# Attention's output: a first sum and difference in halves at four places, and one rotation of queries moved

## Chip, cores, metric

One core of one Trainium2 chip. The time is device microseconds of one execution of the whole program, a single launch; the kernel before has three runs. The five engines are PE (TensorE matmul; PEld are its weight loads), DVE (VectorE), ACT (ScalarE), POOL (GpSimd) and SP (SyncE, which issues most transfers).

## The reference, cut to what matters

The program is four layers over x of 64 sequences of 32 tokens of 512. The change lies in the third layer's attention; the others are untouched.

```python
q = jnp.einsum('bsd,ed->bse', x, Wq).reshape(bsz, seqlen, HQ, D)   # 32 query heads of 128
k = ...                                                            # 8 key heads
v = ...
q = _rope(_rmsnorm(q, q_norm_w), pos)
k = _rope(_rmsnorm(k, k_norm_w), pos)
kc = k_cache[block_table].reshape(bsz, L, HK, D)                   # 512 cached keys per sequence
...
scores = jnp.where(valid[:, None, None, :], jnp.einsum('bqhd,bkhd->bhqk', q, k_all) * SCALE, -1e+30)
probs = jax.nn.softmax(scores, axis=-1)
o = jnp.einsum('bhqk,bkhd->bqhd', probs, v_all).reshape(bsz, seqlen, HQ * D)
return jnp.einsum('bse,de->bsd', o, Wo)
```

## The kernel before, in words

All arithmetic is in fp32. The 2048 tokens are 16 tiles of 128 rows (four sequences each). Attention runs over two halves of the heads, and in each half over the 16 tiles: 32 steps. Two steps make a pair, 16 pairs in all (0 to 15). A step has 16 turns (four sequences times four key heads), a pair 32 turns, and a turn two half steps, so that a pair has half steps 0 to 63.

A turn i does this: PE transposes the probabilities of turn i (`prT_ps`, four matmuls, L1094), and ACT copies them (`prT`, L1423). PE forms the scores of turn i+2 (L1401). DVE adds the mask and takes the minimum (L1406), ACT takes the exponent (L1410), DVE the reciprocal of the sum (L1412), and DVE scales the probabilities (`pr`, L1415). PE multiplies the values with the transposed probabilities (`po`, L1099). Once per sequence DVE forms a mask (L1393) and copies the sequence's own keys (`kt`, L1119), and POOL issues four indirect gathers of values (`vt`, L1125). After two sequences `own_part` adds the tokens' own values and writes the output of four heads' groups into `oT`, a tile of 128 x 16 x 128 per step (L1462 to L1465, on ACT and DVE).

Between these steps two other products are spread over a pair's half steps, by lists of places in the code. `at(i, f)` puts a function at half step i.

- The projections of the next pair (`Projections`): three groups g (keys and values, then two of queries) of seven products m each, in the order 1, 2, 5, 6, 3, 7, 4. Two tiles are taken together as two-by-two blocks with seven products instead of eight. Where a product completes 512 columns of queries or keys, they are normed and rotated (`rotated`): a square on ACT (L1158), on DVE a reduction (L1161), a scaling (L1162) and three multiplications (L1176 twice, L1179), on POOL an addition (L1180), a power (L130) and a multiplication (L1181). For queries the rotation is put off by `WAIT[m]` half steps (`put_off`). Later PE transposes the result (`turned`, L1094, `qkT_ps`), at half steps 37, 43, 51, 53 and so on.
- The output projection of the pair before (`Outputs`), again with seven products over two tiles. With o11, o12 the two halves of the first tile's heads, and o21, o22 those of the second, the products need o21 + o22 (`o_sum`, first read by m = 5 at half steps 16 and 17), later o_sum - o11 and o12 - that (`next_sum`, on DVE, at 17 and 26), and o11 - o21, which is written over o21 (read by m = 7 at half steps 32 and 33). Each operand has 128 x 8 x 128 numbers, and each product runs as two halves u of four of the eight. The first sum and difference are `first_sums` (L1331 and L1332), on POOL, at half step 0 of the next pair. After the last pair they are on DVE.

```python
WAIT = {2: 2, 3: 0, 7: 2, 4: 4}
...
ats = ((2, 4, 10, 12, 14, 18, 20), (22, 28, 30, 34, 36, 38, 40), (42, 44, 46, 50, 52, 54, 58))
...
at(i, partial(p.product, g, m), partial(later.append, next_wp))
```

These lists give the order in which the code issues its instructions. PE's order is tied to it (`on_pe`). On the other engines the framework that the kernel is written in plans the order itself, from the dependencies and buffers and with the code's order as priority, except where `issue_after` ties an instruction behind another: the square of a rotation is tied behind the last prT copy issued before it. Tiles come from pools with a number of buffers (`oT` three, `o_sum` one, masks two, tables of cosines and sines two of each name).

Of the kernel before, what the change touches and what calls it, by code (L numbers as in the profile page):

```python
# [28 lines left out]
ALU = mybir.AluOpType  # L29
# [1024 lines left out]
def attention(c, known, x_in, y_part, y_out, sums, tail):  # L1054
# [15 lines left out]
    tc, nc, a = c.tc, c.nc, c.a  # L1070
    half = HD // 2
    n_c = L // P
    with ExitStack() as outer:
# [64 lines left out]
        WAIT = {2: 2, 3: 0, 7: 2, 4: 4}  # L1138
# [62 lines left out]
        class Projections:  # L1201
# [76 lines left out]
            def turned(self, g, i, n):  # L1278
                r = self.c.pop((g, i, n)).rearrange("p (h d) -> p h d", d=HD)
                pt = transposes("tq", "qkT_ps", [r[:, m, :] for m in range(REP)])  # L1280
                if g == 0:
                    self.kT[i] = qp.tile([P, HKP, P], F32, name="kT_own", bufs=3)
                    nc.scalar.copy(self.kT[i], pt)
                    return
                if i not in self.qT:
                    self.qT[i] = qp.tile([P, HKP, SEQ, REP, S], F32, name="qT", bufs=3)
                nc.scalar.copy(self.qT[i][:, 2 * (g - 1) + n].rearrange("p j h s -> p h j s"),
                               pt.rearrange("p h (j s) -> p h j s", j=SEQ))
# [3 lines left out]
        KH = HQP // 2  # L1292
        QH = KH // 2
# [21 lines left out]
        class Outputs:  # L1315
# [7 lines left out]
            def first_blocks(self):  # L1323
                self.blocks = [(o[:, :KH, :], o[:, KH:, :]) for o in (oTs[2 * self.n],)]

            def first_sums(self, engine):
                self.o = [oTs.pop(2 * self.n + i) for i in range(2)]
                (_, _), (o21, o22) = self.blocks = [(o[:, :KH, :], o[:, KH:, :]) for o in self.o]
                self.s = qp.tile([P, KH, P], F32, name="o_sum", bufs=1)
                for q in (slice(0, KH),) if engine is nc.gpsimd else (slice(0, QH), slice(QH, KH)):  # L1330
                    engine.tensor_tensor(self.s[:, q], o21[:, q], o22[:, q], ALU.add)  # L1331
                engine.tensor_tensor(o21, self.blocks[0][0], o21, ALU.subtract)  # L1332

            def next_sum(self, m, u):
                (o11, o12), _ = self.blocks
# [148 lines left out]
        per = SEQ * HKP  # L1484
        GROUPS = tuple(range(HKP))

        def of(i):
            s, j, g = turns[i]
            h, T = steps[s]
            return s, h, SEQ * T + j, g  # L1490
# [31 lines left out]
        later, to_come, waiting = [], {}, {}  # L1522
# [91 lines left out]
        for s, (h, T) in enumerate(steps):  # L1614
            if s:
                oTs[s] = qp.tile([P, HQP, P], F32, name="oT", bufs=3)
            slots = [[] for _ in range(2 * per)]
            n = s // 2
            last_pair = n == len(outputs) - 1

            def at(i, *fs):
                to_come.setdefault(s * 2 * per + i, []).extend(fs)

            if s % 2 == 0:
                if s == 0:
                    p = projections[0]
                    at(1, partial(p.turned, 2, 0, 1), partial(own_keys, 0, 1, p.kT[0]))
                    for i, f in zip((3, 7, 11, 15), held):  # L1630
                        at(i, f)
                    for i, what in ((13, (1, 1, 1)), (15, (1, 1, 0)), (19, (2, 1, 1)), (25, (2, 1, 0))):
                        at(i, partial(p.turned, *what))
                if not last_pair:
                    p = projections[n + 1]
                    if n == 0:
                        ats = ((12, 14, 16, 17, 18, 20, 22), (24, 26, 28, 32, 33, 34, 38),
                               (40, 42, 44, 48, 49, 52, 56))
                        then = ((0, 0, 0, 21), (0, 1, 0, 29))
                        for i, f in zip((3, 5, 6, 7, 10), (partial(p.x, 0), partial(p.x, 1), p.x_sums,  # L1640
                                                           partial(p.tables, "k"), partial(p.tables, "q"))):
                            at(i, f)
                    else:
                        ats = ((2, 4, 10, 12, 14, 18, 20), (22, 28, 30, 34, 36, 38, 40),
                               (42, 44, 46, 50, 52, 54, 58))
                        then = ((0, 0, 0, 13), (0, 1, 0, 27))
                        at(3, partial(p.tables, "q"))
                    for *what, i in (*then, (1, 0, 0, 37), (1, 0, 1, 43), (1, 1, 1, 51), (1, 1, 0, 53),
                                     (2, 0, 0, 57), (2, 0, 1, 65), (2, 1, 1, 67), (2, 1, 0, 73)):
                        at(i, partial(p.turned, *what))  # L1650
                    for g in range(GB):
                        for m, i in zip(p.ORDER, ats[g]):
                            at(i, partial(p.product, g, m), partial(later.append, next_wp))
                            if g and m != 1 and m != 5 and m != 6:
                                at(i, partial(put_off, s * 2 * per + i + 1 + WAIT[m], waiting))
                    if n + 2 < len(projections):
                        then = projections[n + 2]
                        for i, f in zip((30, 40, 59, 61, 62), (then.load, partial(then.tables, "k"),
                                                               partial(then.x, 0), partial(then.x, 1),
                                                               then.x_sums)):  # L1660
                            at(i, f)
                else:
                    for i, f in zip((6, 14, 38, 46, 54), tail.weights(xp, wk, op, wp_tile)):
                        at(i, f)
                    at(43, tail.scaled)
                    for m, i in enumerate((45, 48, 49, 61)):
                        at(i, partial(tail.fold, ps, m))
                    at(44, begin_tail)
                    at(58, partial(load_tail, "y", 2, 4))
                    for i, tag in enumerate(("sc", "pt")):  # L1670
                        at(62, partial(turn_tail, i, tag))
                    at(52, outputs[n].first_blocks)
                    for i, where in enumerate((52, 54, 57, 59)):
                        at(where, partial(outputs[n].product, i), partial(later.append, next_wo))
                if n:
                    out = outputs[n - 1]
                    at(0, partial(out.first_sums, nc.gpsimd))
                    if out.h:
                        at(14, out.befores)
                    ats = (0, 1, 5, 9, 13, 16, 17, 21, 25, 29, 32, 33, 37, 41) if last_pair else \  # L1680
                        (0, 1, 6, 8, 16, 17, 24, 26, 32, 33, 48, 49, 56, 60)
                    for i, where in enumerate(ats):
                        at(where, partial(out.product, i), partial(later.append, next_wo))
                        if i in (5, 7):
                            for u in range(2):
                                at(where, partial(out.next_sum, 6 if i == 5 else 3, u))
                    at(47 if last_pair else 63, out.store)
                else:
                    for i in (40, 46, 52, 58):
                        at(i, next_wo)  # L1690
            for at in range(2 * per):
                slots[at].extend(to_come.pop(s * 2 * per + at, []))
            for t in range(per):
                i = s * per + t
                _, _, b, g = of(i)
                if last_pair and not prTs:
                    prTs[:] = [qp.tile([P, D], F32, name="projected", bufs=6).rearrange("p (n k) -> p n k", k=P)
                               for _ in range(2)]
                prT = turned(i)
                if g == HKP - 1:  # L1700
                    own_prTs = ([] if b % 2 == 0 else own_prTs) + [own_turned(b)]
                slot(waiting.pop(2 * i, []) + slots[2 * t])
                start(i + 2)
                if g == 1:

                    keys_of(i - 1 + 2 * HKP)
                slot(waiting.pop(2 * i + 1, []) + slots[2 * t + 1])
                to_finish.append(partial(finish, s, i, b, g, prT, own_prTs))
                while len(to_finish) > int(last_pair and i + 1 < len(turns)):
                    to_finish.pop(0)()  # L1710
        out = outputs[-1]
        out.befores()
        out.first_sums(nc.vector)
        load_tail("x", 0, 1)
        for i, tag in enumerate(("sc", "pt")):
            tail.choose(i, tag)
# [540 lines left out]
```

## Time and profile before

| | us |
|---|---|
| median of 3 runs | 3447.67 |
| lowest, highest | 3445.36, 3448.77 |
| the profiled execution | 3450.86 |
| its span, first to last instruction | 3449.1 |
| PE busy | 3402.2 (99%) |
| DVE, ACT, POOL busy | 2184.1, 1626.7, 1650.1 |
| POOL: the first sum, 15 times | 2.36 each (median) |
| POOL: the first difference, 15 times | 2.34 each (median) |
| DVE: mask, 128 times | 0.50 median, 3.01 longest |

The granted TensorE clock was 1.0. Attention's turns begin at 1033 us and end at about 3277 us. Busy times are of one execution; matmuls overlap one another, so that PE's share says that it hardly ever stands still, not that it could do no more. In the lists of groups a line of `at(...)` never shows: the line given is that of the helper which issues the instruction (L1094 for transposes, L1099 for products, L130 for the power).

### The profile page before, as it was taken

Reading aid. Unit: us, or ns where it says so; the run is one execution under the profiler, and the core shown is the slowest. Engines: PE = TensorE matmul, PEld = TensorE weight load, DVE = VectorE, ACT = ScalarE, POOL = GpSimd, SP = SyncE. Lnnn points to the kernel's source line nnn. Section 1 sums busy time; section 2 is a strip of 40 time slices with the busy share of each in tenths; the row PEclk is TensorE's granted clock in tenths of the full one; section 3 lists DMA queues with packets and bytes.
Section 4 is the critical chain, followed back from the end, with each engine's and each line's share of the span. In section 5 each row is a group of like instructions: output and inputs, shape, how many; then the busy total and the mean of one; then the engine's idle time right before and its main releaser. Section 6 shows DMA issues by size and latency. Waiting matters only on the chain.

```text
span 3449.1 us, 66979 instructions
## 1 busy us (share of the span) xinstructions
PE 3402.2 (99%) x21124; PEld 2673.1 (78%) x21124; DVE 2184.1 (63%) x5432; ACT 1626.7 (47%) x4260; POOL 1650.1 (48%) x1647
## 2 busy tenths in 40 slices
PE   8999999999999999999999999999999999999999
PEld 6556888888857777778787777777877778777788
DVE  5454534334457676766767767677676777767477
ACT  6332222222226655555555555555555555555522
POOL 0112433333337655655556455565564655645233
PEclk9999999999999999999999999999999999999999
DMA  5013555545467888888887888878788888887731
GB/s 211 25 52 122 191 160 169 167 156 163 149 224 227 251 255 247 260 262 252 259 256 255 256 252 260 260 252 270 247 256 269 256 265 259 254 255 241 253 104 63
DMA packets 631937, 740.28 MB, mean 215 GB/s; under 512 B 64546, under 2 KB 480290, under 8 KB 631586
## 3 DMA queue, kind: packets, MB, share of 16 engines
q1 hardware_dynamic: 580130, 562.94, 52.4%
q0 software_dynamic: 51456, 173.05, 14.3%
q8 instruction: 172, 2.82, 0.3%
q14 instruction: 179, 1.47, 0.1%
HBM read 689.61 MB, written 46.14 MB: 213 GB/s over the span
## 4 chain that ended last, share of the span: by engine, by line
PE 84%; DVE 6%; DMA 4%; issue 3%; ACT 1%; SPq 1%; POOL 1%; DVEq 0%; POOLq 0%; ACTq 0%
PE po L1099 12%; PE sc L1401 11%; PE py L1099 10%; PE pq L1099 9%; PE prT_ps L1094 6%; PE pkv L1099 5%; PE pz L615 4%; PE pd L276 4%; PE acc_a L615 4%; PE acc L1839 3%; PE acc_c L615 2%; PE qkT_ps L1094 2%; PE po L615 1%; PE acc_b L615 1%; PE acc_a L281 1%
## 5 line engine op out<-in xcount | busy, mean ns | idle before, releaser
L1125 POOL DMA_INDIRECT vt<-in_v_rows,v_rows x512 | 516.5, 1009 | 312.2 <-PE po L1099 187.4
L1410 ACT ACTIVATE pr<-pr,low 128x544 f32<-128x544 f32 x512 | 383.3, 749 | 543.8 <-DVE low L1406 541.9
L1401 PE MATMUL sc<-kt,qT 128*128 128x288 f32 (+1 forms) x2048 | 554.2, 393 | 8.1 <-DMA kt<-in_kT 4.9
L1401 PEld LDWEIGHTS sc<-kt,qT 128*128 128x128 f32 x2048 | 384.4, 190 | 222.5 <-issue 127.5
L1099 PE MATMUL po<-prT,vt 128*128 128x128 f32 x3840 | 508.6, 275 | 2.2 <-ACT prT L1423 0.6
L1099 PEld LDWEIGHTS po<-prT,vt 128*128 128x128 f32 x3840 | 488.4, 192 | 27.6 <-ACT prT L1423 10.6
L1406 DVE CUSTOM_DVE_ANT_0 pr<-sc,mask 128x544 f32<-128x544 f32 x512 | 368.4, 720 | 143.7 <-PE sc L1401 143.5
L1180 POOL TENSOR_TENSOR projected<-projected,swapped 128x512 f32<-128x512 f32 x160 | 208.5, 1303 | 297.4 <-DVE projected L1179 274.9
L1415 DVE TENSOR_SCALAR pr<-pr,low 128x512 f32<-128x512 f32 x512 | 319.5, 624 | 12.6
L1094 PE MATMUL prT_ps<-ident,pr 128*128 128x128 f32 x2048 | 311.4, 275 | 4.9 <-DVE pr L1415 4.8
L1423 ACT COPY prT<-prT_ps 128x512 f32<-128x512 f32 x480 | 275.6, 574 | 18.7 <-PE prT_ps L1094 11.3
L1412 DVE RECIPROCAL low<-low 128x1 f32<-128x1 f32 x512 | 82.2, 160 | 319.2 <-ACT pr L1410 318.6
L1094 PEld LDWEIGHTS prT_ps<-ident,pr 128*128 128x128 f32 x2048 | 236.7, 141 | 15.4 <-issue 7.2
L1099 PE MATMUL py<-wo,oT 128*128 128x256 f32 x1024 | 241.8, 379 | 0.0
L1099 PE MATMUL pq<-wp,x_sums 128*128 128x512 f32 x512 | 240.2, 593 | 0.0
L1099 PEld LDWEIGHTS py<-wo,oT 128*128 128x128 f32 x1024 | 186.4, 190 | 21.1
L130 POOL TENSOR_TENSOR rs<-rs,minus_half 128x4 f32<-128x4 f32 x160 | 179.9, 1125 | 30.3 <-DVE low L1412 18.8
L1413 ACT ACTIVATE own_pr<-pr,low 128x32 f32<-128x32 f32 x512 | 164.9, 322 | 43.8 <-DVE low L1412 40.9
L1099 PE MATMUL pq<-wp,xT 128*128 128x512 f32 x384 | 180.6, 593 | 1.1 <-DVE projected L1269 1.1
L1099 PE MATMUL py<-wo,o_sum 128*128 128x256 f32 x768 | 181.2, 379 | 0.2 <-issue 0.2
L1132 ACT COPY own_vt<-v 32x128 f32<-32x128 f32 x512 | 150.8, 295 | 58.0 <-PE po L1099 42.4
L1181 POOL TENSOR_TENSOR projected<-projected,rs 128x512 f32<-128x512 f32 x160 | 172.0, 1075 | 8.1
(378 smaller groups left out, 6529.9 us busy)
## 6 DMA issues: line engine op xcount, KB each, us to landing
kt<-in_kT SPq DMA_DIRECT2D x2048, 64.0 KB
wp<-in_sums SPq DMA_DIRECT2D x192, 512.0 KB
wo<-out_sums SPq DMA_DIRECT2D x128, 512.0 KB
wp<-in_WqT SPq DMA_DIRECT2D x96, 512.0 KB
wo<-in_WoT SPq DMA_DIRECT2D x96, 512.0 KB
down1T<-in_down1T SPq DMA_DIRECT2D x80, 256.0 KB
wp<-in_WkT SPq DMA_DIRECT2D x32, 512.0 KB
xt<-x SPq DMA_DIRECT2D x48, 256.0 KB
```

The lines of the kernel that those rows point to most:

```text
L130: self.nc.gpsimd.tensor_tensor(t, t, self.minus_half[:, :n], ALU.pow)
L615: c.on_pe(nc.tensor.matmul(out, lhsT, rhs, start=start, stop=stop, skip_group_check=more))
L1094: c.on_pe(nc.tensor.transpose(pt[:, m, :], piece, c.ident))
L1099: c.on_pe(nc.tensor.matmul(out, lhsT, rhs, start=first and i == 0, stop=last and i == len(pairs) - 1))
L1125: nc.gpsimd.indirect_dma_start(out=vts[b % 2][:, n, :], out_offset=None, in_=a["v_rows"], in_offset=bass.IndirectOffsetOnAxis(ap=rows[h][: ...
L1180: last_turn.append(nc.gpsimd.tensor_tensor(src, src, tmp, ALU.add).ins)
L1181: last_scaled.append(nc.gpsimd.tensor_tensor(src, src, rs.unsqueeze(2).to_broadcast([P, REP, HD]), ALU.mult).ins)
L1401: c.on_pe(nc.tensor.matmul(sc[:, lo + n * PSIZE:lo + m * PSIZE].rearrange("p (n k) -> p n k", k=PSIZE), q, kt[:, n:m, g, :], start=True, s ...
L1406: ins = nc.vector.tensor_tensor_reduce(pr[:, :NK], sc[:, lo:lo + NK], masks[h, b], -SCALE, 3.0e38, ALU.add, ALU.min, low[:, 0:1]).ins
L1410: nc.scalar.activation(pr[:, :NK], pr[:, :NK], AF.Exp, bias=low[:, 0:1], scale=-1.0, accum_out=low[:, 1:2])
L1415: nc.vector.tensor_scalar(pr[:, :L], pr[:, :L], low[:, 2:3], None, ALU.mult)
L1423: last_prT.append(nc.scalar.copy(prT, pt).ins)
```

## The change

The first sum and the first difference are each formed in two halves of four of the eight blocks, as separate functions, and put at half steps 2 and 5 (sums) and 19 and 22 (differences) instead of both whole at half step 0. After the last pair, on DVE, the difference is formed in halves too. Beside it, the rotation of the queries that product (g, m) = (1, 3) completes is put off by two half steps instead of none (to half step 39 instead of 37), in all pairs but the first (and the last, which has no projections).

```diff
-            def first_sums(self, engine):
+            def all_blocks(self):
                 self.o = [oTs.pop(2 * self.n + i) for i in range(2)]
-                (_, _), (o21, o22) = self.blocks = [(o[:, :KH, :], o[:, KH:, :]) for o in self.o]
+                self.blocks = [(o[:, :KH, :], o[:, KH:, :]) for o in self.o]
                 self.s = qp.tile([P, KH, P], F32, name="o_sum", bufs=1)
-                for q in (slice(0, KH),) if engine is nc.gpsimd else (slice(0, QH), slice(QH, KH)):
-                    engine.tensor_tensor(self.s[:, q], o21[:, q], o22[:, q], ALU.add)
-                engine.tensor_tensor(o21, self.blocks[0][0], o21, ALU.subtract)
+
+            def first_sum(self, u, engine):
+                o21, o22 = self.blocks[1]
+                q = slice(u * QH, (u + 1) * QH)
+                engine.tensor_tensor(self.s[:, q], o21[:, q], o22[:, q], ALU.add)
+
+            def first_difference(self, u, engine):
+                q = slice(u * QH, (u + 1) * QH)
+                engine.tensor_tensor(self.blocks[1][0][:, q], self.blocks[0][0][:, q], self.blocks[1][0][:, q],
+                                     ALU.subtract)
...
-                                at(i, partial(put_off, s * 2 * per + i + 1 + WAIT[m], waiting))
+                                wait = 2 if n and (g, m) == (1, 3) else WAIT[m]
+                                at(i, partial(put_off, s * 2 * per + i + 1 + wait, waiting))
...
-                    at(0, partial(out.first_sums, nc.gpsimd))
+                    at(0, out.all_blocks)
+                    for u in range(2):
+                        at(2 + 3 * u, partial(out.first_sum, u, nc.gpsimd))
+                        at(19 + 3 * u, partial(out.first_difference, u, nc.gpsimd))
...
         out.befores()
-        out.first_sums(nc.vector)
+        out.all_blocks()
+        for u in range(2):
+            out.first_sum(u, nc.vector)
+        for u in range(2):
+            out.first_difference(u, nc.vector)
```

## Prediction, made before the changed kernel ran

> **What bounds the kernel now.** I read the page first: the busy times, then the chain that ended last.
>
> ```profile
> span 3449.1 us, 66979 instructions
> PE 3402.2 (99%) x21124; PEld 2673.1 (78%) x21124; DVE 2184.1 (63%) x5432; ACT 1626.7 (47%) x4260; POOL 1650.1 (48%) x1647
> PE 84%; DVE 6%; DMA 4%; issue 3%; ACT 1%; SPq 1%; POOL 1%; DVEq 0%; POOLq 0%; ACTq 0%
> ```
>
> PE's work is the time; the change touches none of it. VectorE (DVE) and GpSimd (POOL) count only where they make PE wait. So I asked for PE's waits from 1162 to 3151 us, the attention's pairs 1 to 14 (pairs 0 to 15 have 32 turns each; a pair takes 141.9 to 142.3 us, so one of its 64 half steps about 2.2 us), and again for pair 15, 3151 to 3280 us.
>
> ```profile
> PE prT_ps L1094 <- DVE pr L1415: 1.3, 5, 0.3
> ```
> ```profile
> PE sc L1401 <- DMA kt<-in_kT: 4.9, 2, 3.1
> PE po L1099 <- DVE oT L1465: 2.2, 3, 0.7
> PE prT_ps L1094 <- DVE pr L1415: 1.8, 1, 1.8
> ```
>
> The transposes of the probabilities wait for L1415 five times in pairs 1 to 14 (by their start times: pairs 10 to 14, turn 3) and once in pair 15. The timeline at such a place, pair 12, DVE, POOL, weight loads (PEld) and PE mixed:
>
> ```profile
> 2734.10 2.36 POOL L1331 TENSOR_TENSOR o_sum<-oT 128x1024 f32<-128x1024 f32 x1
> ...
> 2735.37 1.19 DVE L1119 COPY kt<-kT_own 128x128 f32<-128x128 f32 x1
> ...
> 2736.42 0.45 POOL L1221 TENSOR_TENSOR q_cos<-q_norm_row,cos 128x128 f32<-128x128 f32 x1
> 2736.48 3.00 DVE L1393 TENSOR_SCALAR mask<-keys,lens_f 128x544 f32<-128x544 f32 x1
> 2736.83 2.34 POOL L1332 TENSOR_TENSOR oT<-oT 128x1024 f32<-128x1024 f32 x1
> ...
> 2739.40 0.15 DVE L1412 RECIPROCAL low<-low 128x1 f32<-128x1 f32 x1
> 2739.58 0.49 DVE L1415 TENSOR_SCALAR pr<-pr,low 128x512 f32<-128x512 f32 x1
> ...
> 2740.18 0.42 PEld L1094 LDWEIGHTS prT_ps<-ident,pr 128*128 128x128 f32 x4 [0.40 <-issue]
> ```
>
> The mask, 0.50 us at its median, takes 3.00 and ends 0.3 after the difference does; the reciprocal and L1415 queue behind it, and the transposes' weights load 0.40 late. The mask takes 3.00 in twelve of the fourteen pairs, but in pair 4 L1415 ends at 1603.47 and the loads begin at 1603.58: nothing is lost, and nothing is to spare. In pair 15 L1415 itself is caught:
>
> ```profile
> 3157.64 3.93 DVE L1415 TENSOR_SCALAR pr<-pr,low 128x512 f32<-128x512 f32 x1
> ...
> 3157.92 1.05 POOL L1181 TENSOR_TENSOR projected<-projected,rs 128x512 f32<-128x512 f32 x1
> ...
> 3158.92 2.35 POOL L1331 TENSOR_TENSOR o_sum<-oT 128x1024 f32<-128x1024 f32 x1
> ...
> 3161.35 2.44 POOL L1332 TENSOR_TENSOR oT<-oT 128x1024 f32<-128x1024 f32 x1
> ```
>
> It needs 0.49 and ends at 3161.57, 0.3 after the sum; the loads behind it wait 1.92 us.
>
> **The change part by part.** *Sum and difference in halves.* Removed per pair: 2.36 + 2.34 = 4.70 us of POOL. Added: four instructions of 128x512. Between the POOL rows of 256 elements (x_sums, 0.72 us) and 1024 (2.36) a straight line gives 0.72 + 256 x 1.64/768 = 1.27 each, and L1180 (512 elements, 1.26 undisturbed) is beside it: 5.08, or 0.38 us more per pair on an engine busy 48%. That costs nothing unless DVE waits for it; then it is 14 x 0.38 = 5.3.
>
> What it gives: in pair 12 the first half would run 2734.10 to 2735.37, q_cos to 2735.8, the second to 2737.1. If the mask gets in there, it is done 2 us earlier, L1415 has one half at most (1.27) ahead of it, ends by 2738.9 instead of 2740.07, and the 0.40 is gone: 5 x 0.40 = 2.0 us over pairs 10 to 14, nothing in pairs 1 to 9. In pair 15 L1415 gets in after the first half, at 3160.19 instead of 3161.27: 1.1 of the 1.92. Together 3.1 us. The upper bound of this part is both stalls whole, 3.9.
>
> Whether DVE gets in between two POOL instructions that follow without a gap, the trace answers both ways. For: at 1586.79 an L1415 of 0.80 ends inside the second of two touching x_sums instructions, which takes 0.92 instead of 0.73; the COPY above ends just after the sum while q_cos is already running. Against: the mask does not get in between q_cos and the difference, nor L1415 between L1181 and the sum. I take "in", since two dense operands behind each other, as the halves will be, is the x_sums row; the other value is the second rival below.
>
> [...]
>
> *Places.* The halves stand at half steps 2, 5, 19 and 22. The order on an engine isn't the code's alone: the tables that L1221 forms for the next pair's keys are put at half step 40, and k_sin starts at 1606.25, 17.2 us into pair 4, half step 7, as soon as its buffer is free.
>
> ```profile
> 1600.22 2.34 POOL L1332 TENSOR_TENSOR oT<-oT 128x1024 f32<-128x1024 f32 x1
> 1606.25 0.97 POOL L1221 TENSOR_TENSOR k_sin<-k_norm_swapped,sin 128x128 f32<-128x128 f32 x1 [3.69 <-DVE rs L1162]
> ```
>
> The four halves have their inputs from the pair's start, so the last three may well run in that 3.69 us gap and not where they are written. If the differences do run at 19 and 22, the COPY, mask and rotation beside them wait up to 1.27; by L1415's ends and the transposes' starts in pair 4 the cover there is 2.85, 1.92 and 1.62 us (turns 10 to 12): nothing. Without that cover it would be 1.27 per pair.
>
> *The rotation two half steps later*, in pairs 1 to 14: one square on ScalarE (ACT), five DVE instructions, three on POOL (L1180, L130, L1181), no DMA. The square is tied behind the last prT copy, in pair 4 the one at 1675.43 instead of the one before: it moves from 1674.16 to about 1676.4, L1181's end from 1680.11 to 1682.3 at most. Its transposes start at 1685.48: cover 5.4 us now, 3.2 after; cost nothing. Queued behind these POOL instructions are four gathers for values (start to start 1.35, 1.26, 1.25, the last 1.18: 5.04), and on ACT and DVE the next turn's exponent and evictions with 0.87 us of cover at turn 21. With that gone, it is what the third and fourth cases price.
>
> *The tail.* On DVE, after the last pair, the difference of 1.22 becomes two of 0.68: 0.14, beside PE's products of m = 4, 5, 6: nothing.
>
> Sum: -2.0 - 1.1 = -3.1 us. The profiled execution took 3450.86 (span 3449.1 and 1.8 around it) and becomes 3447.8; it lies 3.2 above the median, which becomes 3447.67 - 3.1, about 3444.5. This case's own range is 3442.5 to 3447.
>
> **The rivals.** *Both recurring stalls go* (3437 to 3441). In turn 23 of every pair po's loads wait for the prT copy, which queues behind an exponent that waits for DVE:
>
> ```profile
> 1694.23 0.86 PEld L1099 LDWEIGHTS po<-prT,vt 128*128 128x128 f32 x7 [0.52 <-ACT prT L1423]
> ```
>
> Scores to po is 0.49 between starts, where 0.21 is usual, and the po after it loses another 0.10: 0.38 x 14 = 5.3. DVE is late there because three rotations' POOL work (L1180 at 1686.35 and 1690.57, L1181 at 1687.69) holds its COPY for 1.37 and L1162 for 0.86; the rotation that moves is the one ahead of them. With the 3.9 above: 9.2 less, 3438.5. Against it: moving a rotation later adds to that crowd rather than thinning it.
>
> *The change doesn't do what it says* (3447 to 3456): the four halves run back to back and DVE gets in nowhere, as at q_cos. They end 0.38 later, at no spare time in turn 3: 14 x 0.38 = 5.3; in pair 15 no gap is left (3161.27 to 3161.35 was one, since the difference waited for the sum), so L1415 waits for all four, 3158.92 + 5.08, 2.7 later. Up to 8.0 slower, 3455.7; about 3450 if DVE gets in before the last half, but L1415 doesn't.
>
> *Slower by one mechanism: the rotation falls behind the gathers* (3455 to 3469). If POOL takes the four gathers before L130, which then starts at 1685.2 instead of 1677.95, L1181 ends at about 1687.3, and the transposes due at 1685.48 wait 1.8: up to 25 us in 14 pairs, less what later stalls absorb; I price it at 0.6 to 1.5 a pair. It decides as soon as more than two gathers go ahead (3.2 of cover, 1.26 each). For it: the gather at 1680.27 starts 0.16 after L1181, so it was kept waiting by POOL alone. Against it: the code issues the rotation before the gathers.
>
> **How the numbers follow.** Chances: the forecast 0.30, both stalls 0.26, back to back 0.27, behind the gathers 0.17. The measurement tells 0.2% from no change, 6.9 us: 3440.8 to 3454.6. Faster: both stalls 0.26, and 0.04 of the forecast in case some of turn 23 goes with it: 0.30. Slower: the gathers 0.17 and 0.11 of back to back: 0.28. Same: 0.42. The range, 3437 to 3460, holds the first three cases and the lower part of the fourth.
>
> **What would show it.** Right: four POOL groups of about 1.27 us where two of 2.36 stood, no mask of 3.00, PE's wait for L1415 down from 1.3 to near 0 in pairs 1 to 14 and from 1.8 to about 0.7 in pair 15, and turn 23 as before. Back to back: the halves in one run after L1181 and masks of 3 us still. Both stalls: PEld's wait of po for the prT copy gone. The gathers: PE waiting for L1181 at qkT_ps. I am wrong if PE's waits shrink and the time doesn't, or if a wait stands in turns that the change does not touch.

## Result: 1.7% slower, and the profile after

| | before | after |
|---|---|---|
| median, 5 runs each on the same chip | 3448.73 us | 3509.24 us |
| lowest, highest | 3445.36, 3449.67 | 3505.03, 3514.08 |
| span of the profiled execution | 3449.1 | 3507.8 |

The ratio is 1.0172, 95% interval 1.0161 to 1.0183: 60.5 us slower, where 3444.5 was forecast and the range ended at 3460. From the page of after, the span, the busy times and the chain that ended last:

```profile
span 3507.8 us, 67068 instructions
PE 3414.5 (97%) x21124; PEld 2673.7 (76%) x21124; DVE 2224.8 (63%) x5433; ACT 1626.1 (46%) x4260; POOL 1653.4 (47%) x1677
PE 79%; DVE 8%; DMA 5%; issue 4%; ACT 2%; POOL 1%; SPq 1%; DVEq 0%; POOLq 0%; ACTq 0%
```

POOL's busy time grew by 3.3 us and PE's by 12; the span grew by 58.7. So no engine has become the bound: PE waits more often. DVE's share of the chain went from 6% to 8% with 41 us more of busy time, on the same work: its instructions take longer. (Lines behind the change are numbered 7 higher than before: scores L1408, mask L1400, L1422 for L1415; the sum is L1334, the difference L1338.) PE's waits in pairs 1 to 14, 1164 to 3206 us, and then in pair 15 (total us, times, longest):

```profile
PE prT_ps L1094 <- DVE pr L1422: 30.3, 27, 2.9
PE qkT_ps L1094 <- POOL projected L1181: 13.8, 14, 1.0
PE po L1099 <- ACT prT L1430: 2.4, 15, 0.2
```
```profile
PE prT_ps L1094 <- DVE pr L1422: 4.3, 1, 4.3
```

1.3 us has become 30.3, 1.8 has become 4.3, and the second line is new: once per pair the transposes of the moved rotation wait for its last POOL instruction. How long each pair takes, from its first transposes to those of the next, in the profiled executions (pair 15 to its last turn; it holds waits for the keys' transfer that differ between executions, 4.9 us in before and 0.8 with the rotation alone). The kernels below the second row are the experiments:

| | pair 2 | 3 to 9, each | 10 to 13, each | 14 | 15 |
|---|---|---|---|---|---|
| before | 141.97 | 141.92 | 142.31 | 141.94 | 121.25 |
| after | 149.49 | 145.52 | 145.91 | 145.56 | 124.63 |
| halves alone | 147.88 | 142.40 | 142.79 | 142.40 | 124.54 |
| rotation alone | 145.07 | 145.06 | 145.43 | 145.06 | 118.81 |
| rotation, gathers behind it | 142.07 | 142.05 | 142.44 | 143.28 | 119.07 |
| halves placed | 141.87 | 141.87 | 141.87 | 141.47 | 125.36 |
| sum and difference alternate | 141.88 | 142.02 | 142.31 | 141.94 | 119.16 |
| halves placed, pair 15 alternating | 141.87 | 141.87 | 141.87 | 141.49 | 118.94 |
| whole difference placed | 141.94 | 141.87 | 141.86 | 141.49 | 118.50 |

**The halves.** In pair 4 the four of them begin 8.46, 10.09, 11.33 and 12.55 us into the pair (q_cos between the first two), not at half steps 2, 5, 19 and 22: the planner has put all four right behind the pair's first L1181, which ends at 8.51. Pair 15 of after, timeline of POOL and DVE (start, duration):

```profile
3212.57 6.47 DVE L1422 TENSOR_SCALAR pr<-pr,low 128x512 f32<-128x512 f32 x1
3212.84 1.05 POOL L1181 TENSOR_TENSOR projected<-projected,rs 128x512 f32<-128x512 f32 x1
3213.84 2.48 POOL L1334 TENSOR_TENSOR o_sum<-oT 128x512 f32<-128x512 f32 x2
3216.28 2.47 POOL L1338 TENSOR_TENSOR oT<-oT 128x512 f32<-128x512 f32 x2
```

L1422 needs 0.49 and takes 6.47: it comes while POOL issues a gather (1.02 us from 3211.78), and waits through L1181 and all four halves. Pair 2 is the costlier case. First before (one line of DVE, one of POOL), then after:

```profile
1311.34 4.32 DVE L1415 TENSOR_SCALAR pr<-pr,low 128x512 f32<-128x512 f32 x1
1313.01 2.36 POOL L1331 TENSOR_TENSOR o_sum<-oT 128x1024 f32<-128x1024 f32 x1
```
```profile
1315.59 7.28 DVE L1422 TENSOR_SCALAR pr<-pr,low 128x512 f32<-128x512 f32 x1
```

Already before, L1415 was shut out for 4.32 us there; it ended at 1315.66 and its transposes began at 1315.81, so no wait showed. With 7.28 PE stands still for 2.9 us. In turn 3 of the other pairs it is the COPY of the keys (L1119) that is caught (3.77 to 4.21 us in pairs 3 to 14, 0.22 at its median), then the chain behind it: 0.48 per pair.

**The rotation.** Pair 4 before, POOL, then after, turn 21 and on, POOL, DVE and PE:

```profile
1677.95 1.04 POOL L130 TENSOR_TENSOR rs<-rs,minus_half 128x4 f32<-128x4 f32 x1
1679.07 1.04 POOL L1181 TENSOR_TENSOR projected<-projected,rs 128x512 f32<-128x512 f32 x1
1680.27 1.05 POOL L1125 DMA_INDIRECT vt<-in_v_rows,v_rows  x1 [0.16 <-issue]
```
```profile
1694.07 0.97 POOL L1125 DMA_INDIRECT vt<-in_v_rows,v_rows  x1 [8.67 <-PE po L1099]
1695.35 1.30 POOL L1125 DMA_INDIRECT vt<-in_v_rows,v_rows  x1 [0.30 <-issue]
1696.67 1.04 POOL L130 TENSOR_TENSOR rs<-rs,minus_half 128x4 f32<-128x4 f32 x1
1697.90 1.02 POOL L1125 DMA_INDIRECT vt<-in_v_rows,v_rows  x1 [0.19 <-issue]
1698.95 1.28 POOL L1180 TENSOR_TENSOR projected<-projected,swapped 128x512 f32<-128x512 f32 x1
1700.39 0.97 POOL L1125 DMA_INDIRECT vt<-in_v_rows,v_rows  x1 [0.17 <-issue]
1701.38 1.06 POOL L1181 TENSOR_TENSOR projected<-projected,rs 128x512 f32<-128x512 f32 x1
1702.38 1.51 POOL L130 TENSOR_TENSOR rs<-rs,minus_half 128x4 f32<-128x4 f32 x1
1702.49 0.66 PE L1094 MATMUL qkT_ps<-ident,projected 128*128 128x128 f32 x4 [0.98 <-POOL projected L1181]
1703.31 2.11 DVE L1422 TENSOR_SCALAR pr<-pr,low 128x512 f32<-128x512 f32 x1
1703.88 1.25 POOL L1180 TENSOR_TENSOR projected<-projected,swapped 128x512 f32<-128x512 f32 x1
1705.21 1.10 POOL L1181 TENSOR_TENSOR projected<-projected,rs 128x512 f32<-128x512 f32 x1
1705.56 0.63 PE L1094 MATMUL prT_ps<-ident,pr 128*128 128x128 f32 x4 [1.53 <-DVE pr L1422]
```

The rotation's three POOL instructions (L130, L1180, L1181) now stand among the four gathers, two of which go ahead of all three and all of which ahead of L1181, which ends at 1702.44, 98.0 us into the pair, where before it ended at 91.1. The transposes start 1.15 us late by the matmuls' starts. Right behind it, without a gap, POOL begins the next rotation (L130 at 1702.38), and that shuts out L1422 (2.11 instead of 0.49), for which the next transposes wait another 1.69. Together 2.84 per pair in one turn; 0.2 more is lost in turn 23.

### The profile page after: what moved, and what is told of

Same layout as the page of the kernel before. It is cut to its first block, busy times and chain, and to the rows that moved or that the text cites. A ratio compares the mean times of both kernels' runs of the same rounds, so it can differ in the third digit from the quotient of the medians.

```text
span 3507.8 us, 67068 instructions
## 1 busy us (share of the span) xinstructions
PE 3414.5 (97%) x21124; PEld 2673.7 (76%) x21124; DVE 2224.8 (63%) x5433; ACT 1626.1 (46%) x4260; POOL 1653.4 (47%) x1677
## 4 chain that ended last, share of the span: by engine, by line
PE 79%; DVE 8%; DMA 5%; issue 4%; ACT 2%; POOL 1%; SPq 1%; DVEq 0%; POOLq 0%; ACTq 0%
PE po L1099 11%; PE sc L1408 11%; PE py L1099 10%; PE pq L1099 8%; PE prT_ps L1094 6%; PE pkv L1099 4%; PE pz L615 4%; PE acc_a L615 4%; PE pd L276 4%; PE acc L1854 3%; PE acc_c L615 2%; PE qkT_ps L1094 1%; PE po L615 1%; PE acc_b L615 1%; DVE kt L1119 1%
## 5 line engine op out<-in xcount | busy, mean ns | idle before, releaser
L1408 PE MATMUL sc<-kt,qT 128*128 128x288 f32 (+1 forms) x2048 | 556.5, 394 | 6.9 <-DMA kt<-in_kT 3.7
L1408 PEld LDWEIGHTS sc<-kt,qT 128*128 128x128 f32 x2048 | 384.2, 190 | 224.1 <-issue 118.6
L1422 DVE TENSOR_SCALAR pr<-pr,low 128x512 f32<-128x512 f32 x512 | 337.4, 659 | 12.6
L1180 POOL TENSOR_TENSOR projected<-projected,swapped 128x512 f32<-128x512 f32 x160 | 206.0, 1288 | 228.6 <-DVE projected L1179 201.6
L1420 ACT ACTIVATE own_pr<-pr,low 128x32 f32<-128x32 f32 x512 | 164.6, 322 | 94.1 <-DVE low L1419 93.0
L130 POOL TENSOR_TENSOR rs<-rs,minus_half 128x4 f32<-128x4 f32 x160 | 186.4, 1165 | 28.9 <-DVE low L1419 19.0
L1181 POOL TENSOR_TENSOR projected<-projected,rs 128x512 f32<-128x512 f32 x160 | 168.9, 1055 | 7.2
```

Source lines behind the costliest of these rows:

```text
L130: self.nc.gpsimd.tensor_tensor(t, t, self.minus_half[:, :n], ALU.pow)
L1180: last_turn.append(nc.gpsimd.tensor_tensor(src, src, tmp, ALU.add).ins)
L1181: last_scaled.append(nc.gpsimd.tensor_tensor(src, src, rs.unsqueeze(2).to_broadcast([P, REP, HD]), ALU.mult).ins)
L1408: c.on_pe(nc.tensor.matmul(sc[:, lo + n * PSIZE:lo + m * PSIZE].rearrange("p (n k) -> p n k", k=PSIZE), q, kt[:, n:m, g, :], start=True, s ...
L1422: nc.vector.tensor_scalar(pr[:, :L], pr[:, :L], low[:, 2:3], None, ALU.mult)
```

## The experiments

All ratios are against the kernel before, run beside them on the same chip; the medians of before were 3450.74 us beside experiments 1 to 4, 3453.69 beside 5 to 8 and 3450.40 beside 9 to 11.

**1. The halves alone** (after, with the rotation's wait as before).

```diff
-                                wait = 2 if n and (g, m) == (1, 3) else WAIT[m]
+                                wait = WAIT[m]
```

> The halves alone: the change without the moved rotation (the rotation of (1, 3) is put off by none again). Theory A (the two parts add up; the four halves run back to back on POOL and leave DVE no gap): turn 3 keeps a stall of about 0.48 us in each of 14 pairs, pair 2 its 3 to 4 us, pair 15 about 3.4 more, together about +14 us, 3463, and turn 21 has no stall. Theory B (the halves cost nothing, all of the +60 us comes with the rotation): 3449, within 3 us. Theory C (the halves let DVE in, as forecast): 3444 to 3446.

Measured 3466.95 us, ratio 1.0049 [1.0032, 1.0065]: 16.2 us. By pairs: 5.9 in pair 2, 0.47 in each of pairs 3 to 14 (5.6), 3.3 in pair 15 (5.1 at its stall, less what a shorter wait for the keys gives back), 14.8 in all; the other 1.4 I could not place.

**2. The rotation alone** (before, with one line of the change).

```diff
+                                wait = 2 if n and (g, m) == (1, 3) else WAIT[m]
-                                at(i, partial(put_off, s * 2 * per + i + 1 + WAIT[m], waiting))
+                                at(i, partial(put_off, s * 2 * per + i + 1 + wait, waiting))
```

> The moved rotation alone: the kernel before with the rotation of (1, 3) put off by two half steps. Theory A (the rotation's POOL work falls among the four gathers): the two stalls of turn 21, 1.15 and 1.69 us, and a little at turn 23, about 3.1 us in each of 14 pairs, 3492; turn 3 as before. Theory B (the stalls of turn 21 need the halves too): 3450 to 3455.

Measured 3493.75 us, ratio 1.0129 [1.0112, 1.0145]: 43.0 us, 3.1 in each of pairs 1 to 14. With the 16.2 of the halves that is 59.2 of the 60.5: the parts add up. PE's waits in pairs 1 to 14:

```profile
PE prT_ps L1094 <- DVE pr L1415: 22.7, 19, 1.5
PE qkT_ps L1094 <- POOL projected L1181: 13.7, 14, 1.0
```

**3. The rotation later, its gathers tied behind its L1181** (the lines of 2, and these).

```diff
             if g == HKP - 1:
-                values_of(i - g + 2 * HKP)
+                late = s % 2 and 1 < s < len(steps) - 2 and i % per == HKP - 1
+                with tc.issue_after(last_scaled[-1]) if late else nullcontext():
+                    values_of(i - g + 2 * HKP)
```

> The moved rotation alone, with the four gathers of turn 19 tied behind the rotation's last POOL instruction. Theory A (what costs is that POOL takes gathers first and mixes the rotation with them): 3448 to 3453, no wait of PE for L1181. Theory B (what costs is that the square and so the whole rotation is later): still 3480 to 3495, with the wait for L1181 at turn 21.

Measured 3453.11 us, ratio 1.0008 [0.9998, 1.0017]. 40.6 of the 43 us are gone with the rotation as late as in 2; what cost them was the order on POOL. Not all is gone: turn 23 takes 0.1 longer in each pair and 1.3 in pair 14, where the scores wait 1.0 us for DVE's minimum.

**4. The halves pinned:** all but the first sum tied behind the L1181 last issued before them, rotation as before.

```diff
-                    for u in range(2):
-                        at(2 + 3 * u, partial(out.first_sum, u, nc.gpsimd))
-                        at(19 + 3 * u, partial(out.first_difference, u, nc.gpsimd))
+                    def tied(f, u):
+                        with tc.issue_after(last_scaled[-1]):
+                            f(u, nc.gpsimd)
+                    at(2, partial(out.first_sum, 0, nc.gpsimd))
+                    at(13, partial(tied, out.first_sum, 1))
+                    for u in range(2):
+                        at(19 + 3 * u, partial(tied, out.first_difference, u))
```

> The halves alone, no moved rotation, and now really apart: the second sum (half step 13) and the two differences (19 and 22) are each tied behind the last rotation of keys that POOL has before them. Theory A (what costs is four POOL instructions without a gap in turns 2 and 3): no mask of 3 us, turn 3 and the stall of pair 15 gone or small, 3443 to 3446. Theory B (halving itself costs, 5.08 us of POOL for 4.70, wherever it stands): 3452 to 3463.

Measured 3453.97 us, ratio 1.0011 [1.0001, 1.002]. Theory A had it below before; by the time alone it would be theory B, halves that cost wherever they stand. The table decides against B: pairs 10 to 13 lost their stall (141.87), pair 2 has none, and pairs 1 to 14 together take 2.8 us less than before. Pair 15 takes 4.1 more: it has no rotation, so nothing to tie to, and its halves run back to back as in the change (L1422 6.49 us).

**5. As 4, with pair 15's halves on DVE.**

```diff
+                    if last_pair:
+                        for u in range(2):
+                            at(2 + u, partial(out.first_sum, u, nc.vector))
+                            at(6 + u, partial(out.first_difference, u, nc.vector))
+                    else:
...
```

> The kernel with the halves pinned behind L1181 by an order of their own (rotation as before), and in pair 15, which has no rotation to pin them to, the four halves on DVE instead of POOL (four of about 0.68 us, as in the tail). Theory A (the cost of the halves is one gapless stretch of POOL in which DVE is shut out; where the stretch is broken up, the forecast's gain is there): the trace of the pinned halves already has pairs 1 to 14 at 2.8 us less than before in sum, and loses 4.1 in pair 15; with pair 15 freed of POOL its stall of 4.5 us and the slow matmuls behind it go, and of the 1.9 that before loses there most goes too: 3445 to 3448 where before is at 3450.7, ratio 0.998 to 0.9995, no PE wait for L1422 over 0.5 us in pairs 1 to 15. Rival B (halves cost by themselves, wherever they are): 3453 or more, as with the halves pinned. Rival C (DVE's own four halves now stand ahead of the normalisation in pair 15): a stall of up to 2.7 us at turn 1 to 2 of pair 15 and 3448 to 3451.

Measured 3454.91 us, ratio 1.0005 [0.9996, 1.0014], no different from before. Pairs 1 to 14 are as in 4; in pair 15 it is the third theory: the sums and differences stand ahead of DVE's minimum, themselves caught by POOL (2.12 and 2.02 us in place of 0.68), and the scores wait 3.5 us for it.

**6. The same four halves on POOL at one place, in the order sum, difference, sum, difference.**

```diff
+                with tc.issue_after(self.half) if u and engine is nc.gpsimd else nullcontext():
                     engine.tensor_tensor(self.s[:, q], o21[:, q], o22[:, q], ALU.add)
...
+                self.half = engine.tensor_tensor(...).ins        # the difference
...
                     for u in range(2):
-                        at(2 + 3 * u, partial(out.first_sum, u, nc.gpsimd))
-                        at(19 + 3 * u, partial(out.first_difference, u, nc.gpsimd))
+                        at(2, partial(out.first_sum, u, nc.gpsimd))
+                        at(2, partial(out.first_difference, u, nc.gpsimd))
```

> The halves on POOL at one place, rotation as before, but in the order sum, difference, sum, difference, so that each difference has to wait for the sum just ahead of it, as the whole difference does in the kernel before; the changed kernel has sum, sum, difference, difference, and no instruction of it waits for the one ahead. Same instructions, same sizes, same crowd. Theory A (DVE gets in only where POOL has a gap, and a gap is where an instruction waits for its predecessor): in pair 15 L1422 gets in behind the first sum, takes about 2.7 us instead of 6.5 and the stall falls from 4.5 to about 0.8; in pair 2 the stall of 3.0 goes; in turn 3 the mask gets in a half earlier and the 0.48 of pairs 3 to 9 goes: 3447 to 3453 where the halves alone took 3467. Rival B (DVE is shut out for as long as POOL has work, gap of 0.08 us or not; or the cost is the 0.38 us that four instructions take more than two): 3462 to 3468, stalls as with the halves alone.

Measured 3453.98 us, ratio 1.0004 [0.9994, 1.0013], where 1 had 1.0049: the same instructions, the same work, 16 us less, each against its own before, by order alone. Pair 15, DVE and POOL (the sum is L1335 here, the difference L1339, the scaling L1423):

```profile
3162.38 1.79 DVE L1423 TENSOR_SCALAR pr<-pr,low 128x512 f32<-128x512 f32 x1
3162.60 1.28 POOL L1335 TENSOR_TENSOR o_sum<-oT 128x512 f32<-128x512 f32 x1
3163.96 1.35 POOL L1339 TENSOR_TENSOR oT<-oT 128x512 f32<-128x512 f32 x1
```

The sum ends at 3163.88, the difference that waits for it starts at 3163.96, and L1423 ends at 3164.17, 0.29 after the sum and with the difference running, which takes 0.08 longer than usual. Counted over the whole trace: of 16 such boundaries (sum, then the difference that waits for it) at which a DVE instruction stood waiting, it got in at 16; of 15 boundaries without that wait (difference, then next sum), at two, both times a COPY. In the changed kernel, sum to difference 0 of 15 and difference to difference 0 of 15.

**7. The rotation one half step later** instead of two, sum and difference as before.

```diff
-                                wait = 2 if n and (g, m) == (1, 3) else WAIT[m]
+                                wait = 1 if n and (g, m) == (1, 3) else WAIT[m]
```

> The kernel before with the rotation of queries moved by one half step instead of two, halves untouched. In POOL's order one gather of the four now stands between L1180 and L1181, where two half steps put two gathers ahead of L180's part and mix the rest. Theory A (the cost sets in when the gathers get ahead of the rotation; the spare time of L1181 before its transposes holds one gather): no PE wait for L1181, 3447 to 3455 where before is at 3450.7. Rival B (the cost goes with the lateness of the rotation, about 1.5 us a pair for each half step): 3468 to 3475, and a wait of the transposes of about half the 1.1 us seen with two half steps.

Measured 3464.04 us, ratio 1.0035 [1.0022, 1.0049]: 10.4 us, between the two theories. The transposes don't wait for L1181, as the first theory had it, but 0.8 us per pair are lost in turn 23, where the scores wait for the minimum.

**8. The whole change with the remedies of 3 and 5** (their two edits, on the changed kernel).

```diff
+                with tc.issue_after(last_scaled[-1]) if late else nullcontext():
...
+                            at(2 + u, partial(out.first_sum, u, nc.vector))
...
+                        at(13, partial(tied, out.first_sum, 1))
```

> The change whole (rotation two half steps later, sum and difference in halves), with both remedies: the gathers behind the rotation's L1181, and the halves pinned behind L1181 with pair 15's on DVE. Theory A (each part's cost is one of order on POOL; no cost is left when both orders are set): 3446 to 3451 where before is at 3450.7 and the changed kernel at 3509; the rotation brings nothing (its own remedy alone gave ratio 1.0008), so about 2 us over the halves placed with the rotation as before. Rival B (the two parts share the engine and meet again, the pinned halves now beside the later rotation): 3455 to 3475, a wait of the transposes at turn 21.

Measured 3480.21 us, ratio 1.0084 [1.0071, 1.0098]: 26.5 us, the rival. The transposes of turn 21 no longer wait; the scores of turn 23 do, 1.4 us per pair, and that turn takes 1.7 longer than before. The remedies of the two parts do not add up as the parts did. In this kernel the prT copy on ACT in turn 22, and with it the next rotation's square, runs 1.5 us later than in 3; why the copy is late stays open.

**9. As 4, with pair 15 on POOL in the order of 6.**

```diff
+                behind = u and engine is nc.gpsimd and self.n == len(outputs) - 2
+                with tc.issue_after(self.half) if behind else nullcontext():
                     engine.tensor_tensor(self.s[:, q], o21[:, q], o22[:, q], ALU.add)
...
+                    if last_pair:
+                        for u in range(2):
+                            at(2, partial(out.first_sum, u, nc.gpsimd))
+                            at(2, partial(out.first_difference, u, nc.gpsimd))
+                    else:
...
```

> The halves pinned behind L1181 in pairs 1 to 14, and in pair 15 on POOL in the order sum, difference, sum, difference; rotation as before. Theory A (DVE gets in only at a gap of POOL; both forms give it one): 2.8 us less than before in pairs 1 to 14, and pair 15 about 2 us less (119.2 against 121.25 in the profiled executions): ratio 0.9982 to 0.9995, the fastest kernel of the study. Rival (the remaining gain is lost again to a transfer that PE waits for in pair 15, or to the spread between executions, which is larger than the gain): 0.9995 to 1.0015.

Measured 3447.07 us against 3450.40, ratio 0.9992 [0.9983, 1.0001]. The profiled span is 3444.7, pairs 1 to 14 are 2.7 us shorter (2.1 of it in turn 3 of pairs 10 to 14) and pair 15 2.3, the transfer's wait included (1.1 of it at the stall). That is the gain which the forecast had written down (2.0 and 1.1), but 0.08% is not to be told from no change by these runs.

**10. The kernel before, with nothing halved:** only the difference, whole, taken away from the sum and pinned behind a later L1181.

```diff
+                if engine is nc.vector or self.n == len(outputs) - 2:
+                    self.first_difference(engine)
...
                     at(0, partial(out.first_sums, nc.gpsimd))
+                    def tied():
+                        with tc.issue_after(last_scaled[-1]):
+                            out.first_difference(nc.gpsimd)
+                    if not last_pair:
+                        at(13, tied)
```

> The kernel before, sum and difference whole (1024 elements each), with the difference alone taken away from the sum and pinned behind a later L1181 in pairs 1 to 14; pair 15 and the rotation as before. Theory A (what helps in turn 3 is that less POOL work touches there; the halving is not needed for it): the stalls of pairs 10 to 14 go as with the halves pinned, no PE wait for L1415 in pairs 1 to 14, ratio 0.9988 to 1.0002. Rival (only short instructions let DVE in, a whole difference of 2.36 us moves the stall to where it now stands): new waits for L1415 or for low, ratio 1.001 to 1.006.

Measured 3448.17 us, ratio 0.9993 [0.9984, 1.0002], pairs 10 to 13 at 141.86: the same as with halves. So no halving is needed; the stall goes when the difference leaves the run of sum and q_cos. In its new place it touches L1181, and there DVE gets in, in 13 of the 13 pairs in which L1420, the scaling of this kernel, stands waiting. Pair 4, POOL and DVE:

```profile
1609.53 1.03 POOL L1181 TENSOR_TENSOR projected<-projected,rs 128x512 f32<-128x512 f32 x1
1609.70 1.15 DVE L1420 TENSOR_SCALAR pr<-pr,low 128x512 f32<-128x512 f32 x1
1610.53 2.54 POOL L1337 TENSOR_TENSOR oT<-oT 128x1024 f32<-128x1024 f32 x1
```

In 4 it is the same at the two places per pair where a tied half follows L1181, in pairs 1 to 13, 26 of 26. Touching alone is therefore not what shuts DVE out.

**11. As 7, with the gathers behind L1181.**

```diff
-                values_of(i - g + 2 * HKP)
+                late = s % 2 and 1 < s < len(steps) - 2 and i % per == HKP - 1
+                with tc.issue_after(last_scaled[-1]) if late else nullcontext():
+                    values_of(i - g + 2 * HKP)
```

> The rotation one half step later, as in the run that gave ratio 1.0035, and its gathers behind L1181. Theory A (the 0.8 us of turn 23 come from the one gather between L1180 and L1181: with it POOL's next rotation runs about 2 us later, and its L1181 falls on L1179, 0.68 to 1.38, right ahead of the scores' eviction): 0.9995 to 1.0015, turn 23 as before. Rival (the later rotation itself changes DVE's and ACT's order at turn 23): 1.0025 to 1.0045, the wait of the scores for low as with one half step alone.

Measured 3461.34 us, ratio 1.0031 [1.0019, 1.0042]: the rival, so the one gather of 7 was not the cause. Pair 4, turn 22, DVE and POOL, and below it the same place in 3:

```profile
1690.07 1.05 POOL L130 TENSOR_TENSOR rs<-rs,minus_half 128x4 f32<-128x4 f32 x1
1690.52 2.13 DVE L1415 TENSOR_SCALAR pr<-pr,low 128x512 f32<-128x512 f32 x1
1691.10 1.25 POOL L1180 TENSOR_TENSOR projected<-projected,swapped 128x512 f32<-128x512 f32 x1
```
```profile
1687.26 0.68 DVE L1415 TENSOR_SCALAR pr<-pr,low 128x512 f32<-128x512 f32 x1
1687.70 1.14 POOL L130 TENSOR_TENSOR rs<-rs,minus_half 128x4 f32<-128x4 f32 x1
```

With the gathers done 0.9 us earlier, the next rotation's power and addition run together just as L1415 comes, and DVE's next minimum comes 0.64 later in the pair than in 3. In 3, L130 comes 0.44 after L1415's start and L1415 takes 0.68. This can be the cause in 11 only: in 7 the minimum comes as late (0.67) though L1415 takes 0.49 there, behind a prT copy that is 0.43 later than in 3. What the two have in common stays open. So 3 is no rule that gathers belong behind rotations; it is one arrangement in which the runs of POOL instructions miss the DVE instructions that count, by tenths of a microsecond.

## Why the prediction was wrong

**"I take 'in'": the step that failed for the halves.** The forecast let DVE in between two halves that follow without a gap. It doesn't get in (0 of 30 in the changed kernel), so the third case, "the change doesn't do what it says", describes what the halves do: back to back, around q_cos, differences waiting for nothing. I chose "in" because two x_sums instructions looked like the halves, against rows that were nearer: the mask between q_cos and the difference, L1415 between L1181 and the sum. Counting the touching boundaries in attention in the trace of before, those at which a DVE instruction had stood waiting for 0.3 us or more (it took over 1.3 times its median), would have said so. Where the POOL instruction that comes next has 256 elements or fewer, as x_sums has, DVE got in at 97 of 97 (between sum and q_cos 13 of 13); where it has 512 or 1024, as a half and the whole have, at 0 of 19 (between q_cos and difference 0 of 12). So the row that I took was of the wrong size. In the changed kernel the same count is 99 of 100 and 0 of 67. The size is a sign and cannot be the whole cause: behind L1181 in 4 and 10 DVE gets in ahead of 512 and 1024 too, in 6 twice between a difference and the next sum, and the one miss, between the first half and q_cos in pair 2, is ahead of 128 (in 6 DVE gets in at that same place). What decides it at a touching boundary stays open.

**The price of that case.** 0.38 per pair measured 0.47, in twelve pairs, and L1422 in pair 15 ended 2.55 later than before by its stall (4.47 against 1.92), where 2.7 was worked out. What isn't in those terms is larger: pair 2, 5.9 us. I had looked for places where PE already waited; in pair 2 it did not, but L1415 of 4.32 us ended only 0.15 before the transposes began. That row, nearly nine times its usual 0.49 without a wait behind it, was a stall that only needed a push: it takes 7.28 in after. And both long stalls were followed by matmuls at half the clock (0.50, below), 1.5 to 3.0 us on top.

**The rotation: "cost nothing" and the fourth case.** L1181 was to end "at 1682.3 at most", 2.2 us later than before; it ended 6.9 later. The premise that failed is that POOL's order stays as it was. The fourth case had it right: more than two gathers' time ahead of L1181, its end at about 1687.3, which is 98.3 us into the pair, against 98.0 measured. Two of its steps were wrong. I cut its 1.8 us of wait to 0.6 to 1.5 for "what later stalls absorb"; nothing was absorbed, the wait was 1.15 and a second one of 1.69 came on top, since the late rotation runs into the next and the two shut DVE out. 14 x 3.1 is 43 us where 25 was the upper end. And the argument against it, the order in which the code issues, did not hold, since the order on POOL is planned; experiment 3, which imposes that order, is where the cost goes away. At 0.17 the case was too unlikely by the profile's own sign, the gather that waited for POOL alone.

**What held.** The halves take 1.27 and 1.26 each, as worked out. They do not run where they are written. No mask of 3.00 is left, but for another reason than forecast: the COPY ahead of it in DVE's queue takes the blow. (Groups of after: busy us, mean ns of one; before, L1119 had a mean of 470 and the mask one of 753.)

```profile
L1119 DVE COPY kt<-kT_own 128x128 f32<-128x128 f32 x128 | 81.9, 640 | 0.0
L1400 DVE TENSOR_SCALAR mask<-keys,lens_f 128x544 f32<-128x544 f32 x128 | 66.2, 518 | 0.0
```

Turn 23 did not gain, so the second case was wrong. The gain in turn 3 and pair 15 exists, and at the forecast's size: kernel 9 has both in its trace, kernel 10 that of turn 3. The change just didn't reach it, since its places bind nothing.

**How long DVE is shut out.** The wait can last over several POOL instructions that follow without a gap: L1422 in pair 2 of after took 7.28 us over six of them (L1181, both halves of the sum with q_cos between them, both of the difference). At other touching boundaries DVE got in, in before at the 97 of 97 counted above.

## What to carry to other kernels

Here POOL shut DVE out, and a run of its instructions without a gap could count as one (7.28 us over six): cutting long ones into touching pieces made it worse (16.2 us in 1), while putting them apart (DVE in at 26 of 26 boundaries in 4), or ordering them so that each difference waits for the sum just before (16 of 16 in 6), let DVE in. A row that showed DVE getting in spoke at best for pieces of its own size (97 of 97 ahead of 256 elements or fewer, 0 of 19 ahead of 512 or 1024). Before moving work on an engine whose order is planned, find out what the planner will put in its place, and pin what must hold by an explicit order; places in the code that bind nothing decided nothing here. And look in the trace of before not only for waits but for instructions far over their usual length which end just in time.

## What the runs showed of the hardware that I had not expected

After a stall of 2.9 us PE came back at half the clock (0.50). Pair 2 of after, in three stretches (length; busy time of PE, PEld, DVE, ACT, POOL; granted clock; DMA share; GB/s): the stall, what follows, and the time after that.

```profile
1319.90:1323.10 3.20, 0.35 (x4) 0.19 (x3) 3.20 (x2) 0.00 (x0) 2.69 (x3) 0.92 0.79 196
1323.10:1325.80 2.70, 2.70 (x7) 1.67 (x8) 1.62 (x6) 1.81 (x5) 0.00 (x0) 0.50 0.90 298
1325.80:1329.00 3.20, 3.20 (x20) 2.52 (x19) 2.03 (x5) 0.86 (x2) 0.00 (x0) 0.97 0.56 140
```

At a clock of 0.50 the matmuls of 128 columns came 0.10 us further apart and those of 512 columns 0.43, 1.5 us in this pair and 3.0 with the halves alone. It isn't the length of the stall alone: in before PE waits 3.1 us at 3236 and has a clock of 1.00 behind it, and in pair 15 the same stall of 1.8 us is followed by 1.00 in before and by a stretch of 0.50 with the rotation alone. First the rotation alone, then before:

```profile
3204.78:3208.19 3.41, 1.66 (x10) 1.23 (x9) 3.41 (x4) 1.00 (x3) 3.33 (x2) 1.00 1.08 350
3208.19:3211.60 3.41, 3.41 (x10) 2.70 (x9) 2.43 (x8) 1.50 (x5) 0.55 (x1) 0.50 0.47 120
```
```profile
3159.80:3163.20 3.40, 1.64 (x10) 1.19 (x9) 3.40 (x4) 0.96 (x3) 3.32 (x2) 1.00 1.09 350
3163.20:3166.60 3.40, 3.40 (x24) 3.17 (x23) 2.44 (x7) 1.52 (x4) 0.58 (x1) 1.00 0.50 128
```

The half clock lasts 3.41 us here and begins 1.5 us after PE has taken up work again. In the 3.41 us ahead of it PE was busy for 1.66 at a clock of 1.00; in before it was busy for 1.64 of 3.40, and no half clock followed. Why the same stall costs this in one execution and not in the other was not shown.
